# A two-layer gated block, float32, on one core: the residual of the local stage kept by tokens, shared single PSUM banks, new step orders

## The chip, the cores and the metric

The kernel runs on one core of one Trainium2 chip, in float32. The metric is the time of one launch in microseconds, as the device measures it; lower is better. The profile is of one execution, with its instructions on TensorE (PE; its weight loads are PEld), VectorE (DVE), ScalarE (ACT), GpSimd (POOL) and SyncE (SP, which here only issues DMAs), and its DMA packets.

## The reference

Sixteen batches of 256 tokens by 128 features go through two layers, each a gated cross-attention and a gated feed-forward part:

```python
x = x + tanh(g_xattn[0]) * cross_attention_0(layernorm(x), ctx)        # 16 heads of 8, causal, 64 keys
x = x + tanh(g_ffn[0])   * local_net(layernorm(x))
x = x + tanh(g_xattn[1]) * cross_attention_1(layernorm(x), ctx)        # 16 heads of 8, with biases
x = x + tanh(g_ffn[1])   * experts(layernorm(x))

def local_net(y):                                   # two of these one after the other
    h = shift_token(y)      # features 64..127 of token n come from token n - 1 (zero for n = 0)
    q, k, v = split(h @ wqkv, 3)                    # 8 heads of 64
    q, k = rotary(l2norm(q) * qs, l2norm(k) * ks)
    y = y + local_attention(q, k, v) @ wo           # windows of 64 that look one window back
    h = layer_norm(shift_token(y)) * lg + lb
    a, g = split(h @ w1 + b1, 2)                    # 341 wide each
    return y + (a * gelu(g)) @ w2 + b2
```

The experts: sigmoid of `x @ router_w.T` for 8 experts, the best two, their weights made to sum to one; each expert is `relu(x @ w1)**2 @ w2`, four of width 128 and four of width 256. All eight are computed for all tokens, and weighed by a table that is zero for those not chosen.

## The kernel before

One step works on one batch b: 256 tokens, held as two tiles of 128 tokens by 128 features. `x_sb` holds the residual of the whole kernel by tokens (a token on each partition). Three stages follow one another, each a set of streams of small steps:

- **Cross stage 0** (0 to 142 us): startup loads and tables (FIRST, REST and TABLE steps), cross-attention of all batches (CROSS_STEPS), and the first layer norms of the local stage (NORM_STEPS, the first EARLY batches).
- **Local stage** (142 to 856 us): attention of layer 0 (LOCAL_STEPS), its GLU (GLU_STEPS), attention of layer 1, its GLU (LAST_GLU_STEPS).
- **Cross stage 1** with the experts (856 to 1163 us): SECOND_STEPS and EXPERT_STEPS. The experts start while the cross-attention still runs.

The order of the work is not written out by hand. A table line such as `project 4 PE 0.5 share M:add` says: step `project`, lag 4, on PE, planned cost 0.5 us, needs `share`, takes a buffer of class M until `add` has run. For each engine the steps are put in the order of (batch + lag), and, among equals, of the table. `timetable()` then plays this once in Python: an engine's next step is placed when its needs have ended and the buffers it takes are free by the planned costs. `play()` issues all instructions in that order. On the chip each engine runs its own instructions strictly in order and waits at each for its data and buffers; so what a table fixes is each engine's order, and which bank a step gets, not when a step runs.

PSUM in the cross stages has three double banks BIG0 to BIG2 (any user takes a free one) and two single banks: M, for `turn`, `query`, `mturn` and `project`, and O, for `mix` and `router`. In the local stage there are QK, SC and TR (double), VB and OB (single), each with fixed users; the GLU maps its own names onto them by GLU_HOMES.

The steps that the change touches (lines of the kernel before):

- Layer norm, `normed` (L915): `stat` (DVE, L922/923: mean and variance), `rstd` (POOL, L927/928), `offset` (DVE, L931: minus mean times rstd), `apply` (POOL, L940: x times rstd plus offset), `turn` (PE, L902: two 128x128 transposes into PSUM), `turn_out` (ACT, L951).
- `first` (L1165): the layer norm in front of the local stage; its `out` (ACT) copies the transposed result into **yT**, the residual of the local stage, held transposed: features on partitions, tokens along the row.
- Local attention: `shift` (SP, L1261/1262) copies yT by two DMAs into one of three `hbuf`, the upper 64 features one token later; `qk` (PE, L1267) and `value` (L1297) read hbuf as stationary operand; `sin`, `cos` (DVE, L1278), `sums` (L1292), `top` (DVE, L1383/1388), `total` (L1404); `rotate`, `clip`, `norm`, `scale`, `share` on POOL (L1312, L1317, L1329-1334, L1340, L1410); `value_out` (DVE, L1304) and `dma` (SP, L1305/1307) build `vbuf`; `project` (PE, L1445: 4 matmuls of 256 columns); `add` (DVE, L1451) adds to yT.
- GLU: `shift` (POOL, L1245/1246) copies yT into one of two `gbuf`, one token later for the upper features; `hturn` (PE, L902) turns that back to tokens; `stat`, `apply` (DVE, L1484/1485, L1495) read it in PSUM; `rstd` (POOL, L1489/1490); `nturn` (PE), `affine` (ACT, L1505), `up0` to `up2` (PE, L1521), `gelu` (ACT, L1531), `gate` (DVE, L1539), `down` (PE, L1545: 3 matmuls of 256 columns), `out` (DVE, L1551: PSUM plus bias plus yT). In the last GLU `yturn` (PE) turns the sum to tokens and `back` (DVE, L1561) adds it, gated, to x_sb.
- Cross-attention: `score` (PE, L1015-1031), `top` (DVE, L1040), `parts` (DVE), `mturn` (PE, L1062), `score_t` (PE, L1078-1092), `exp` (ACT, L1102), `mix` (PE, L1115), `log` and `inverse` (ACT), `refine` and `share` (DVE), `project` (PE, L1145), `add` (DVE, L1152).
- Experts: `hid0` to `hid2` (PE, L1632, a BIG bank each), `relu`, `square` (ACT), `out0`, `out1` (PE, L1654: 12 matmuls each, for one tile of tokens and all experts, into one BIG bank), `sum0`, `sum1` (DVE, L1662: eight 128x128 multiply-adds onto x_sb each, then the store, L1666).

Of the kernel before, what the change touches and what calls it, by code (L numbers as in the profile page):

```python
# [40 lines left out]
exp0 7 ACT 1.08 score_t pT:mix  # L41
mturn 2 PE 0.25 parts M:mturn_out
mturn_out 6 ACT 0.38 mturn mT:score_t
exp1 7 ACT 1.08 score_t,exp0
turn_out 4 ACT 0.38 turn xnT:query
rstd 2 POOL 1.03 stat
vals 5 POOL 0.32 - V:mix
refine 8 DVE 0.84 inverse
share 8 DVE 0.43 refine oT:project
log 7 ACT 0.38 mix  # L50
stat 2 DVE 0.92 - sm:apply
offset 3 DVE 0.16 rstd
top0 5 DVE 1.2 score
apply 2 POOL 1.02 offset xn:turn
score 1 PE 1.25 query_out,keys BIG:top0 BIG:top1
turn 0 PE 0.4 apply M:turn_out
keys 3 POOL 0.6 - Kd:score+score_t
mix 3 PE 1.8 exp0,exp1,vals O:share
inverse 7 ACT 0.38 log
top1 5 DVE 1.2 score,top0  # L60
parts 5 DVE 0.9 top0,top1 mp:mturn
add 8 DVE 0.48 project
query 0 PE 0.6 turn_out M:query_out
query_out 4 ACT 0.39 query QT:score+score_t
score_t 2 PE 1.2 mturn_out,query_out,keys BIG:exp0 BIG:exp1
project 4 PE 0.5 share M:add
# [3 lines left out]
inverse 6 ACT 0.38 log  # L70
score 6 PE 1.25 query_out,keys BIG:top0 BIG:top1
apply 1 POOL 1.02 offset xn:turn
stat 3 DVE 0.92 - sm:apply
turn 5 PE 0.4 apply M:turn_out
top0 6 DVE 1.2 score
exp0 5 ACT 1.08 score_t pT:mix
mturn_out 4 ACT 0.38 mturn mT:score_t
exp1 5 ACT 1.08 score_t,exp0
mix 8 PE 1.8 exp0,exp1,vals O:share
rstd 0 POOL 1.03 stat  # L80
top1 6 DVE 1.2 score,top0
parts 6 DVE 0.9 top0,top1 mp:mturn
keys 0 POOL 0.6 - Kd:score+score_t
query 5 PE 0.6 turn_out M:query_out
offset 4 DVE 0.16 rstd
add 9 DVE 0.48 project
turn_out 2 ACT 0.38 turn xnT:query
score_t 7 PE 1.2 mturn_out,query_out,keys BIG:exp0 BIG:exp1
refine 8 DVE 0.84 inverse
share 8 DVE 0.43 refine oT:project  # L90
log 5 ACT 0.38 mix
vals 2 POOL 0.32 - V:mix
project 9 PE 0.5 share M:add
query_out 2 ACT 0.39 query QT:score+score_t
mturn 6 PE 0.25 parts M:mturn_out
# [3 lines left out]
hid2 4 PE 1.88 turn_out,hid1 BIG:relu2  # L99
stat 4 DVE 0.92 -  # L100
hid0 3 PE 1.88 turn_out BIG:relu0
prob 8 ACT 0.22 router
rstd 0 POOL 0.95 stat
apply 0 POOL 0.9 offset exn:turn
relu1 7 ACT 1.06 hid1,relu0
# [333 lines left out]
def flamingo_kernel(ctx: ExitStack, tc: tile.TileContext, a: dict, out: bass.AP):  # L439
# [518 lines left out]
    def cross(layer, small, wp, pp):  # L958
# [203 lines left out]
        )  # L1162


    def first(small, wp, pp, xn_tag, acc):  # L1165

        live = {}

# [610 lines left out]
```

## Time and profile before

| | |
|---|---|
| median of 3 runs | 1164.57 us (1163.31 to 1165.63) |
| the profiled execution | 1164.6 us, its span 1162.8 us |
| granted PE clock, mean | 0.989 |

| stage | from | to | us per batch in the steady part |
|---|---|---|---|
| cross stage 0 | 0 | 142 | 7.23 |
| attention, layer 0 | 142 | 427 | 16.18 |
| GLU 0 | 427 | 491 | 5.05 |
| attention, layer 1 | 491 | 775 | 15.72 |
| GLU 1 | 775 | 857 | 5.28 |
| cross-attention 1 | 857 | 950 | 6.74 |
| experts | 950 | 1163 | 11.49 |

The span runs from the first instruction to the last; around it lie the 1.8 us by which the execution's own time is longer. The time per batch is taken between equal steps of neighbouring batches in the trace. A row of a timeline gives the start, the busy time, the engine, the line, the operation with its tiles and shapes, and in square brackets how long the engine stood idle before and whose work ended that. A busy PE is not a PE at its peak, since the ends of pipelined matmuls are modelled.

### The profile page before, as it was taken

The page shows a single profiled execution, that of the slowest core. Times are in us where ns is not written, and L with a number is a line of the kernel's source. Part 1 is how long each engine was busy: PE and PEld are TensorE (multiplying, and loading weights), DVE is VectorE, ACT ScalarE, POOL GpSimd, SP SyncE. Part 2 cuts the span into 40 slices and gives each one's busy share as a digit, 9 for nine tenths or more (in the row PEclk, how much of TensorE's full clock was granted, in tenths as well). Part 3 has the DMA queues.
Part 4 walks back from the last instruction along what each step waited for, and adds up shares of the span by engine and source line. Part 5 has one row for each costly group of instructions (what it writes and reads, how often), then busy time and mean ns, then how long its engine had stood idle before and what let it go on. Part 6 is the DMA issues. An engine that isn't in the chain of part 4 may idle for free.

```text
span 1162.8 us, 28289 instructions
## 1 busy us (share of the span) xinstructions
PE 1080.4 (93%) x11264; PEld 786.3 (68%) x11264; DVE 940.2 (81%) x2088; ACT 734.9 (63%) x1418; POOL 630.9 (54%) x1079
## 2 busy tenths in 40 slices
PE   7999878999999999888999999999979999999997
PEld 5555535766767777655667767677645557999996
DVE  7887679999999856679999999856757884777777
ACT  4555447888888863357888888853335557555462
POOL 5443179999988833258888888733345460111110
PEclk9999989999999999999999999999989999999999
DMA  6400011111111100001111111100000000000000
GB/s 182 143 2 2 10 24 33 33 29 38 37 31 36 29 10 10 1 14 33 37 30 37 38 34 33 29 7 1 1 1 2 2 1 2 12 13 12 13 12 17
DMA packets 29828, 30.02 MB, mean 26 GB/s; under 512 B 4668, under 2 KB 22656, under 8 KB 29696
## 3 DMA queue, kind: packets, MB, share of 16 engines
q1 hardware_dynamic: 28352, 27.56, 9.4%
q8 instruction: 89, 1.46, 0.5%
q10 hardware_dynamic: 1344, 0.66, 0.2%
q14 instruction: 43, 0.35, 0.1%
HBM read 9.33 MB, written 2.10 MB: 10 GB/s over the span
## 4 chain that ended last, share of the span: by engine, by line
PE 70%; DVE 18%; ACT 6%; issue 4%; POOL 1%; DMA 1%; SPq 0%; DVEq 0%; ACTq 0%; POOLq 0%
PE QK L1267 8%; PE e_y L1654 8%; PE e_h_ps L1632 7%; PE po L1115 5%; PE Ag L1521 4%; PE OB L1427 4%; PE TR L1415 3%; PE SC L1374 3%; ACT pr L1397 3%; DVE mx L1383 3%; PE VB L1297 3%; PE OB L1445 3%; PE TR L1346 3%; DVE qn L1278 3%; PE sT L1092 2%
## 5 line engine op out<-in xcount | busy, mean ns | idle before, releaser
L1397 ACT ACTIVATE pr<-SC,mx,rn 128x128 f32<-128x128 f32 x512 | 185.6, 468 | 36.1 <-DVE mx L1388 36.0
L1267 PE MATMUL QK<-wqkv,hbuf 128*128 128x512 f32 x256 | 129.5, 629 | 19.3 <-DVE qn L1278 14.2
L1410 POOL TENSOR_TENSOR pr<-pr,rs 128x1024 f32<-128x1024 f32 x64 | 121.4, 1896 | 14.7 <-DVE rs L1405 11.4
L1662 DVE SCALAR_TENSOR_TENSOR x_sb<-e_y,e_comb,x_sb 128x128 f32<-128x128 f32 x256 | 89.1, 349 | 21.6 <-PE e_y L1654 13.7
L1644 ACT ACTIVATE e_h<-e_h_ps 128x1024 f32<-128x1024 f32 x48 | 49.2, 1025 | 77.2 <-PE e_y L1654 61.8
L1267 PEld LDWEIGHTS QK<-wqkv,hbuf 128*128 128x128 f32 x256 | 44.6, 193 | 77.8 <-issue 40.2
L1654 PE MATMUL e_y<-mw,e_h 128*128 128x128 f32 x768 | 91.8, 277 | 0.0
L1632 PE MATMUL e_h_ps<-e_xnT,mw 128*128 128x256 f32 x384 | 89.8, 383 | 0.2
L1654 PEld LDWEIGHTS e_y<-mw,e_h 128*128 128x128 f32 x768 | 89.2, 192 | 0.7
L1040 DVE TENSOR_REDUCE nm<-sc 128x16 f32<-128x1024 f32 x64 | 75.0, 1214 | 14.2 <-PE sc L1031 14.0
L1275 ACT ACTIVATE sq<-QK 128x1024 f32<-128x1024 f32 x64 | 65.9, 1030 | 31.8 <-ACT pr L1397 9.0
L1312 POOL TENSOR_TENSOR qn<-qn,u 128x512 f32<-128x512 f32 x64 | 81.3, 1271 | 8.6 <-DVE qn L1278 6.0
L1278 DVE TENSOR_TENSOR u<-QK,tab 128x1024 f32<-128x1024 f32 x64 | 76.9, 1201 | 9.3 <-ACT sq L1275 5.4
L1102 ACT ACTIVATE xpT<-sT,penT 128x1024 f32<-128x1024 f32 x64 | 71.3, 1117 | 20.3 <-PE sT L1092 20.3
L1404 DVE TENSOR_REDUCE rs<-pr 128x8 f32<-128x1024 f32 x64 | 77.6, 1212 | 7.9 <-ACT pr L1397 5.3
L1383 DVE TENSOR_REDUCE mx<-SC 128x8 f32<-128x1024 f32 x64 | 77.5, 1212 | 6.3 <-PE SC L1374 6.3
L1313 POOL TENSOR_TENSOR qn<-qn,u 128x512 f32<-128x512 f32 x64 | 81.6, 1275 | 0.0
L1418 ACT COPY pT<-TR 128x1024 f32<-128x1024 f32 x64 | 64.4, 1007 | 24.0 <-PE TR L1415 24.0
L1278 DVE TENSOR_TENSOR qn<-QK,tab 128x1024 f32<-128x1024 f32 x64 | 77.6, 1213 | 1.1 <-ACT sq L1275 1.1
L1292 DVE TENSOR_REDUCE ss<-sq 128x16 f32<-128x1024 f32 x64 | 77.1, 1205 | 1.1 <-ACT sq L1275 1.1
L1632 PEld LDWEIGHTS e_h_ps<-e_xnT,mw 128*128 128x128 f32 x384 | 70.4, 190 | 10.9 <-DVE x_sb L1662 2.7
L1531 ACT ACTIVATE hhg<-Ag,cols 128x256 f32<-128x256 f32 x64 | 28.7, 472 | 72.7 <-PE Ag L1521 36.4
(217 smaller groups left out, 2644.8 us busy)
## 6 DMA issues: line engine op xcount, KB each, us to landing
vbuf<-vbuf SPq DMA_DIRECT2D x96, 128.0 KB
hbuf<-yT SPq DMA_DIRECT2D x32, 64.0 KB
out_dram<-x_sb SPq DMA_DIRECT2D x32, 64.0 KB
hbuf<-yT SPq DMA_DIRECT2D x32, 63.8 KB
wqkv<-in_L_ffn_wqkv_dram SPq DMA_DIRECT2D x2, 768.0 KB
mw<-in_L_ffn_w_dram SPq DMA_DIRECT2D x2, 768.0 KB
w<-in_L_ffn_w_dram SPq DMA_DIRECT2D x2, 341.0 KB
x_sb<-in_x_dram SPq DMA_DIRECT2D x1, 640.0 KB
```

The costliest lines, as they stand in the source:

```text
L1267: nc.tensor.matmul(ps[:, 512 * j : 512 * j + 512], lhsT=hbuf[b % 3][:, W + t * P : W + (t + 1) * P], rhs=wqkv[:, l, 512 * j : 512 * j + 51 ...
L1278: nc.vector.tensor_tensor(work(tag, b, t, [P, 2, LH, LD], 2, wp), live["QK", b, t].rearrange("p (q h d) -> p q h d", q=2, h=LH), tab[:, l, ...
L1292: nc.vector.tensor_reduce(ss, live["sq", b, t].rearrange("p (g d) -> p g d", d=LD), AX.X, ALU.add)
L1312: nc.gpsimd.tensor_add(qg[:, :, 0:32], qg[:, :, 0:32], ug[:, :, 32:64])
L1313: nc.gpsimd.tensor_add(qg[:, :, 32:64], qg[:, :, 32:64], ug[:, :, 0:32])
L1383: nc.vector.tensor_reduce(mx, live["SC", b, t].rearrange("p (g c) -> p g c", c=P), AX.X, ALU.max, negate=True,)
L1397: nc.scalar.activation(pr[:, g, :], live["SC", b, t][:, g * P : (g + 1) * P], AF.Exp, bias=live["mx", b, t][:, g : g + 1], scale=live["rn" ...
L1404: nc.vector.tensor_reduce(rs, live["pr", b, t], AX.X, ALU.add)
L1410: nc.gpsimd.tensor_tensor(pr, pr, rs, ALU.mult)
L1632: nc.tensor.matmul(ps[:, c * S : (c + 1) * S], lhsT=mw1[:, (4 * j + c) * P : (4 * j + c + 1) * P], rhs=live["xnT", b], start=True, stop=True,)
L1654: nc.tensor.matmul(y[:, e * D : (e + 1) * D], lhsT=live["h", b][:, c, t * P : (t + 1) * P], rhs=mw2[:, c, :], start=(c == cs[0]), stop=(c ...
L1662: nc.vector.scalar_tensor_tensor(xt, live[f"y{t}", b][:, e * D : (e + 1) * D], live["comb", b][:, t, e : e + 1], xt, ALU.mult, ALU.add,)
```

## The change

- **The residual of the local stage is kept by tokens**, as `y_sb`. `apply` of the first layer norm writes it directly, so `turn` and `out` of that norm go. Attention gets its transposed, shifted input by `hturn` (two transposes on PE into bank VB) and `hout` (two ACT copies of 64 partitions into hbuf) in place of two DMAs. The GLU gets its shifted input by three SP DMAs from y_sb to gbuf in place of two POOL copies; its `hturn` goes, `stat` and `apply` read gbuf, `yturn` goes.
- `project` and `down` swap their operands, so that results come by tokens: 16 instructions of 128 columns for 8 of 256, and 12 for 6 (a float32 matmul is two instructions of the trace). The bias b2 is loaded as a row on all partitions and added by a new POOL step `bias`; `out` is a plain add.
- **Layer norm without `offset`**: POOL's `apply` subtracts the mean and multiplies by rstd.
- **Single banks**: `turn`, `query`, `mturn`, `mix`, `project` and `router` take M or O, whichever is free.
- **Experts' halves**: `out0` to `out3` compute four experts each, in the order out2, out3, out0, out1; `weigh` (DVE, four a batch) multiplies a half with the weights of its experts in one 128x512 instruction, `gather` (POOL) adds the four products (256, then 128 wide) and then x_sb, with the store after every second. They take the place of 16 multiply-adds.
- **All step tables are new** in order, lags and planned costs.

```diff
 CROSS_STEPS = """
...
-mturn 2 PE 0.25 parts M:mturn_out
...
-offset 3 DVE 0.16 rstd
...
-turn 0 PE 0.4 apply M:turn_out
...
-project 4 PE 0.5 share M:add
+project 5 PE 0.57 share M:add
...
+turn 0 PE 0.4 apply M:turn_out
...
 GLU_STEPS = """
...
-shift 6 POOL 1.25 - hg:hturn
-stat 2 DVE 0.92 hturn
-hturn 0 PE 0.44 shift T:apply
...
+bias 6 POOL 0.5 shift
+shift 5 DMA2 2.8 - hg:apply
+stat 0 DVE 0.92 shift
+out 4 DVE 0.48 down,bias
...
-    yT = resid.tile([P, B, S], F32, tag="yT", name="yT")
-    hbuf = [resid.tile([P, W + S], F32, tag=f"hbuf{i}", name=f"hbuf{i}") for i in range(3)]
+    y_sb = resid.tile([P, B, 2, D], F32, tag="y", name="y_sb")
+    hbuf = [resid.tile([P, S], F32, tag=f"hbuf{i}", name=f"hbuf{i}") for i in range(3)]
...
-                    xn[:, t, :], x[:, t, :], live["rstd", b][:, t : t + 1],
-                    live["off", b][:, t : t + 1], ALU.mult, ALU.add,
+                    xn[:, t, :], x[:, t, :], live["mv", b][:, t, 0:1],
+                    live["rstd", b][:, t : t + 1], ALU.subtract, ALU.mult,
...
-        def shift(b, t):
-            h = hbuf[b % 3]
-            nc.sync.dma_start(h[0:64, W : W + S], yT[0:64, b, :])
-            nc.sync.dma_start(h[64:128, W + 1 : W + S], yT[64:128, b, 0 : S - 1])
+        def hturn(b, t):
+            turn(acc("VB", b, t, 512), y_sb[:, b])
+
+        def hout(b, t):
+
+            h, ps = hbuf[b % 3], live["VB", b, t]
+            nc.scalar.copy(h[0:64, :], ps[0:64, 0:S])
+            nc.scalar.copy(h[64:128, 1:S], ps[64:128, 0 : S - 1])
...
         def project(b, t):
             ps = acc("OB", b, t, 512)
-            for r in range(4):
-                nc.tensor.matmul(
-                    ps[:, 0:S], lhsT=wo[:, l, r, :], rhs=live["oT", b, 0][:, r, :],
-                    start=(r == 0), stop=(r == 3),
-                )
+            for t in range(2):
+                for r in range(4):
+                    nc.tensor.matmul(
+                        ps[:, t * P : (t + 1) * P],
+                        lhsT=live["oT", b, 0][:, r, t * P : (t + 1) * P], rhs=wo[:, l, r, :],
+                        start=(r == 0), stop=(r == 3),
+                    )
...
         def shift(b, _):
-            shifted(yT, b, gbuf[b % 2])
...
+            g, y = gbuf[b % 2], y_sb[:, b]
+            nc.sync.dma_start(g[:, :, 0:64], y[:, :, 0:64])
+            nc.sync.dma_start(g[1:P, :, 64:D], y[0 : P - 1, :, 64:D])
+            nc.sync.dma_start(g[0:1, 1, 64:D], y[P - 1 : P, 0, 64:D])
...
+        def bias(b, _):
+            y = y_sb[:, b]
+            nc.gpsimd.tensor_tensor(y, y, b2[:, l].unsqueeze(1).to_broadcast([P, 2, D]), ALU.add)
...
         def out_(b, _):
-            nc.vector.scalar_tensor_tensor(
-                yT[:, b, :], live["B", b][:, 512 : 512 + S], cols[:, 16 + l : 17 + l],
-                yT[:, b, :], ALU.add, ALU.add,
-            )
...
+            y = y_sb[:, b].rearrange("p t d -> p (t d)")
+            nc.vector.tensor_add(y, live["B", b][:, 512 : 512 + S], y)
...
-        def sum_(b, t):
...
+        def weigh(b, j):
+            t, half = j // 2, j % 2
+            nc.vector.tensor_tensor(
+                work(f"w{j}", b, [P, 4, D], 4, wp, tag="e_w"),
+                live[f"y{t}", b][:, 512 * half : 512 * half + 512]
+                .rearrange("p (e d) -> p e d", e=4),
+                live["comb", b][:, t, 4 * half : 4 * half + 4].unsqueeze(2)
+                .to_broadcast([P, 4, D]), ALU.mult,
+            )
+
+        def gather(b, j):
+            w, xt = live[f"w{j}", b], x_sb[:, 2 * b + j // 2, :]
+            nc.gpsimd.tensor_add(w[:, 0:2, :], w[:, 0:2, :], w[:, 2:4, :])
+            nc.gpsimd.tensor_add(w[:, 0, :], w[:, 0, :], w[:, 1, :])
+            nc.gpsimd.tensor_add(xt, xt, w[:, 0, :])
+            if j % 2:
+                nc.sync.dma_start(out_v[:, 2 * b + j // 2, :], xt)
...
-    anywhere = lambda r, b: accs if r == "BIG" else (r,)
+    anywhere = lambda r, b: accs if r == "BIG" else ("M", "O") if r in ("M", "O") else (r,)
```

The orders that come of the new tables, as far as the prediction speaks of them (k is the batch of the round). Cross stage 0, PE: mix k, query k+3, score_t k+1, project k-1, turn k+4, score k+3, mturn k+2. Local attention: `hturn` stands behind `turn0` on PE, `hout` behind `root1` on ACT; POOL runs clip, rotate, share, norm, scale. GLU 0: DVE runs gate0 k, out k-1, gate1 k, apply k+3, gate2 k, stat k+4; PE runs nturn k+1, up2 k-1 ahead of up0 k, up1 k, down k-1. GLU 1: DVE runs gate0 k, back k-2, out k-1, stat k+3, gate1 k, gate2 k, apply k+3; PE runs nturn k+2, up0 k+1, down k, up1 k+1, up2 k+1. At the end of each attention layer DVE runs top0 of batch 15, stat 0, value_out1, add 13, apply 0, stat 1, total0 of batch 15, top1, apply 1, stat 2, apply 2, total1; SP issues shift 0 and shift 1 between the last batch's first and second `vbuf` copies.

## The prediction

> **What bounds the kernel now.** I read five views in this order. First the page's busy line and the shares of the chain that ended last:
>
> ```profile
> PE 1080.4 (93%) x11264; PEld 786.3 (68%) x11264; DVE 940.2 (81%) x2088; ACT 734.9 (63%) x1418; POOL 630.9 (54%) x1079
> ...
> PE 70%; DVE 18%; ACT 6%; issue 4%; POOL 1%; DMA 1%; SPq 0%; DVEq 0%; ACTq 0%; POOLq 0%
> ```
>
> PE carries the end, but not alone. So, second, the table of stretches, one of steady batches per stage (columns: length, then busy PE, PEld, DVE, ACT, POOL, clock, DMA):
>
> ```profile
> 28.26:122.19 93.93, 86.35 (x1431) 51.64 (x1434) 76.31 (x222) 51.16 (x91) 37.16 (x88) 1.00 0.14 48
> ...
> 442.00:482.00 40.00, 36.03 (x176) 29.21 (x175) 25.10 (x80) 14.65 (x32) 13.00 (x32) 1.00 0.01 3
> 790.00:840.00 50.00, 47.22 (x228) 35.22 (x227) 33.94 (x104) 16.27 (x37) 16.69 (x40) 1.00 0.00 1
> 553.15:616.06 62.91, 62.91 (x754) 44.34 (x753) 60.75 (x69) 53.20 (x114) 51.84 (x72) 1.00 0.16 35
> ...
> 1000.00:1140.00 140.00, 139.75 (x952) 129.22 (x951) 103.00 (x432) 75.76 (x97) 20.80 (x46) 1.00 0.04 13
> ```
>
> The first cross stage (first line) leaves PE idle 7.6 of 94 us, GLU 0 (second) 10%, GLU 1 (third) 6%; local attention (fourth) has PE and DVE full together; the experts (last) are PE alone. Third, timelines of one batch show who makes PE wait. In the first cross stage:
>
> ```profile
> 89.90 0.71 PE L1145 MATMUL pw<-wT,oT 128*128 128x128 f32 x4
> 91.19 0.27 PE L1062 MATMUL mT_ps<-ident_bf,mparts 128*128 128x128 bf16 x2 [0.57 <-DVE x_sb L1152]
> ```
>
> `mturn` has all its data, but its bank M is held by `project` until DVE's `add` has read it. GLU 0 has the same picture with bank B and `out`:
>
> ```profile
> 460.23 0.48 DVE L1551 SCALAR_TENSOR_TENSOR yT<-Bg,cols,yT 128x256 f32<-128x256 f32 x1
> ...
> 460.76 1.09 PE L1521 MATMUL Bg<-hnTg,w 128*85 128x256 f32 x4 [0.50 <-DVE yT L1551]
> ```
>
> Among the experts the bank of the first `out` goes to `hid1` only after eight DVE sums, so the second `out` (same 24 instructions) is stretched from 2.68 to 2.94 us until its successor may start; and at the end 24 sums stand behind PE's last matmul, which ends at 1154.2:
>
> ```profile
> 1067.43 2.92 PE L1654 MATMUL e_y<-mw,e_h 128*128 128x128 f32 x24
> 1070.37 1.99 PE L1632 MATMUL e_h_ps<-e_xnT,mw 128*128 128x256 f32 x8
> ```
> ```profile
> 1151.29 8.97 DVE L1662 SCALAR_TENSOR_TENSOR x_sb<-e_y,e_comb,x_sb 128x128 f32<-128x128 f32 x24
> ```
>
> Fourth and fifth, the waits and the DMA records, used below.
>
> **The change, part by part.** Base: the profiled execution, 1164.6 us (span 1162.8 and 1.8 around it); the median, 1164.57, is the same.
>
> *Cross stage 0.* 13 batches take 93.93 us: 7.23 each. With M and O open to any user, `mturn` waits for no `add`. Late next: `turn` takes the bank that `share` frees, so a loop score to tops 2.39, `parts` 1.07, `refine` .91, `share` .40, `turn` .36, `score` 1.42: 6.55, and six handovers of about .03 make 6.75. PE's own work is 6.5, ACT's loop 6.55. Gain .48 x 13 = 6. Bounds: 0 (`share` to `turn` costs what `add` to `mturn` did, the nearest row) to .7 x 13 = 9 (PE dense).
>
> *Start of the local stage.* After the first `qk` at 142.2 PE waits until 148.1 for `n.turn[2]`, behind POOL's `apply`s, each waiting for DVE's `offset`. `apply` now writes y_sb and needs no PE; `hturn` of the first batches has its data from the previous stage. The second `sin` goes from 152.6 to about 149.8 and the third from 160.0 to 155: gain 4 (bounds 0 and 6).
>
> *Local attention.* PE gets `hturn` (two transposes, .25 us by the L902 rows) and `project` 16 x .112 = 1.79 in place of 1.72; ACT gets `hout`, two 64-partition copies, .7 by its 128x256 copies of .38, on 13.3 of 15.7 us, where it idled .8 and .5. The two SP copies to hbuf go. Layer 1 has no spare PE time (62.91 of 62.91) but its 15.72 us contain waits on DVE: I take +.2 x 16 = +3 (bounds 0, +.35). Layer 0 now pays 16.18 a batch (201.81 to 331.29, 8 batches), since `n.turn` and `n.out` run beside it; they go, so does `offset`: -.2 x 8 = -1.5. Sum +1.5, bounds -5 and +8. DVE's L1388 takes .17 us alone and .74 to 1.06 when it ends with POOL's share L1410: the new POOL order (clip, rotate, share, norm, scale) could move that either way by .4 a batch, which is inside the bounds.
>
> *GLU 0.* Bank B is freed by `out`, which no longer stands behind two gates: chain up2, up0, up1 (.87 each), down 1.34, `out` .79 (.2 to its start, .47, .12 back to PE) = 4.74 against 5.05. `down` keeps its time (12 half-width instructions for 6). Gain .31 x 13 = 4.
>
> *GLU 1.* Before, 5.28: `hturn`, `nturn` and `yturn` are three pairs of transposes, and gates queue. After, PE holds nturn .22, three ups 2.61, down 1.34 = 4.17; the loop up1, gelu1, gate1, down, with bank A for up0, about 4.4. Gain .85 x 13 = 11 (bounds 4, 14). POOL's `bias` (128x256, broadcast) .76 by L983 and `rstd` .95 fit in 4.4.
>
> *The GLU's shift.* It was two POOL copies (.39 + .40); now three SP copies with rows of 256 bytes, two buffers. The nearest row is hbuf's second copy, L1262: issue at 201.85, first packet at 203.06, landed at 203.84, 2.0 us. Three issues .5 apart give 1.0 + 1.7 = 2.8 us, and all is hidden. But the second copy has 127 rows. SP's queue shows 3672 packets of 4 bytes, the completion marks. 227 copies with 16 engines each make 3632; the other 40 come out exactly if a copy uses the largest divisor of its row count up to 16: 8 for the router's 8 rows, 7 x 2 and 8 x 1 for the small rows, and 5 (not 16) for each of the two loads of 85 rows. 127 is prime: one engine gets all 254 packets. Packets of 256 bytes follow each other on one engine at 14.3 ns (qk_scale loads); for SBUF to SBUF the 1024-byte packets take 44 ns at first and 70 when all engines run, 1.6 times as long, so 14.3 to 22.7. Landing: .51 + 1.21 + 254 x 14.3 ns + .35 = 5.7 us, or 7.8. I take 5.7, since one engine alone is like the first packets.
>
> Does that hide? On DVE in GLU 0 two periods hold `stat` to the next `apply` but one (3.2 by its rows) and the copy with its two handovers: (3.2 + 5.7 + .25) / 2 = 4.6, under 4.74; in GLU 1 (2.75 + 5.95) / 2 = 4.35, under 4.4. So it is just covered, with no slack. The bound of the engine itself is 254 packets and some .35 for the other two copies: 4.0 at 14.3 ns, 6.1 at 22.7. At the two transitions it is not covered: `stat[0]` and `stat[1]` stand on DVE between the last batch's `top0`, `total0` and `top1`; shift[0] is issued after the last `value_out0` (401.4 + 1.1) and lands at 408.4, shift[1] behind it on the same engine at 412.3, while `total0[15]` started at 410.74: 413.3 now. I take +2.5 each, +5 (bounds 0, +10).
>
> [...] By the nearest row alone (16 engines) the sum below would be 5 lower. [...]
>
> *Transitions otherwise.* GLU 0 to layer 1: a DMA round of 2 us becomes transpose and copy, 1 us: -1. GLU 1 to the second cross stage: `yturn` goes: -1.
>
> *Cross stage 1.* Period 6.74, the same gap at `mturn`; the loop mix, query, score_t, exp0, turn_out, exp1 is 6.45: -.3 x 10, and expert work that starts earlier fills gaps: -4 together (bounds 0, -8).
>
> *Experts.* 11.49 a batch. PE content: 3 `hid` x 1.73, turn .22, router .37, 2 x 2.68 = 11.14. `weigh` (128x512, .69 by L1304 .67) frees a half at once; 4 gathers x 1.3 us (POOL: 256 wide .62, 128 wide .35 twice) = 5.2 fit in 11.1. -.3 x 13 = -4 (bounds 0, -6).
>
> *Tail.* 8.6 us after PE's end become .15 + .69 + 1.3 + up to 1 in a queue + 2.4 for the store (1160.3 to 1162.8) = 5: -3.5.
>
> Sum: -6 - 4 + 1.5 - 4 - 11 + 5 - 2 - 4 - 4 - 3.5 = -32, so 1164.6 - 32 = **1132.6 us**.
>
> **Rivals.**
> 1. *Only the banks fail*: in both cross stages `share` to `turn` takes the place of the wait removed, and the change doesn't do there what it says. The gap of .57 at `mturn` speaks for it, the new order (turn behind project) against. -6 and -3 gone: 1141.6.
> 2. *Local attention pays*: `hturn` takes bank VB between the values, `hout` sits in ACT's row of exps, and the loop DVE to PE lengthens by .6 x 32 = 19, at most what `n.turn` cost layer 0 in its worst cycle, 1.6 us (17.33 against 15.72): 1151.6.
> 3. *The shift binds both GLUs (slower)*: if packets take 22.7 ns, one engine needs 6.1 us a batch: the 15 saved there are lost, (6.1 - 5.05) x 16 + (6.1 - 5.28) x 16 = 30 come on top, and 4 at the transitions: 1132.6 + 15 + 30 + 4 = 1181.6. Break-even: the sum can bear 32 us, 15 by lost gains and 17 by .53 a batch, 5.7 us, from 21 ns on.
> 4. *More comes*: the upper bounds of both cross stages (-3, -4), of the start (-2), of GLU 1 (-3) and the experts (-2), and GLU 0 at PE's own 4.2 (-7): 1111.6.
>
> **Numbers.** Forecast 1132.6 (1123 to 1141 as its own range) .48; rival 1 .12; rival 2 .13; rival 3 .12; rival 4 .15. Range: 1108 (rival 4 and a little) to 1158 (rival 2 with bounds of the local part); outside are rival 3 and a tenth of the rest. .2% (2.3 us) is about what a measurement of this kernel can tell from no change. Faster .86, within .02 (between rivals 2 and 3), slower .12.
>
> **What would show it.** In the new profile: no PE gap at `mturn`, cross period 6.75; GLU periods 4.7 and 4.4, with DVE's `stat` not waiting for a DMA; if it does, rival 3, and the period is the packet count times the packet time. Local cycles within 15.7 to 16.0. DVE's last `weigh` under 1 us after PE's last matmul. I am wrong if the local cycles exceed 16.4, if the copy lands in 3 us, or in more than 7.

## The result and the profile after

The changed kernel takes **1172.49 us** (median of 4 runs, 1170.80 to 1173.91) against 1164.08 us of the kernel before beside it (4 runs): a ratio of 1.006, 95% interval 1.0036 to 1.0084. It is slower, by a little over half a per cent, where 1132.6 was forecast; the time lies above the range. Run once more later (label s9_same, 12 runs), it took 1169.67 us, ratio 1.0032 (1.0019 to 1.0046): slower again.

The page of the changed kernel's profiled execution (span 1170.3 us, before 1162.8) has these lines where the prediction showed those of before; first busy time, then the shares of the chain that ended last:

```profile
PE 1080.1 (92%) x11648; PEld 809.9 (69%) x11648; DVE 897.7 (77%) x1832; ACT 747.3 (64%) x1466; POOL 777.7 (66%) x1239
...
PE 57%; DVE 11%; POOL 7%; DMA 4%; ACT 4%; issue 4%; SPq 2%; POOLq 0%; DVEq 0%; ACTq 0%
```

DVE got 42 us of work less, as meant. But POOL got 147 us more (630.9 to 777.7). The chain after can be followed back no further than 139.65 us, so its shares add up to 89%, and the two lines can't be compared as they stand. Summed from 140 us on in both traces, PE holds 669 us of the chain (696 before) and DVE 124 (199), while POOL, DMA and SP's queue (SPq) hold 148 together, where they held 14. The work was taken from an engine and a wait that were near the bound, and what came in its place got onto the path.

Where the 7.5 us of span went is read between the same steps of both traces (the `add` of a cross stage, the `add` of attention, the GLU's `out`), which leaves nothing over:

| stretch | before, us | after, us | difference | forecast |
|---|---|---|---|---|
| start to the last add of cross stage 0 | 140.7 | 135.2 | -5.5 | -6 |
| to the last add of layer 0 (local start, attention, transition) | 287.9 | 307.1 | **+19.2** | -3 |
| to the last out of GLU 0 | 88.3 | 80.3 | -7.9 | -4 |
| to the last add of layer 1 | 259.7 | 264.7 | +5.0 | +4.5 |
| to the last out of GLU 1 | 78.9 | 72.6 | -6.3 | -11 |
| to the first add of cross stage 1 | 28.8 | 29.7 | +0.9 | -1 |
| to the end (cross stage 1, experts, tail) | 278.6 | 280.7 | **+2.1** | -11.5 |
| sum | 1162.8 | 1170.3 | +7.5 | -32 |

Five groups of lines show why. **One: the clock at the local start.** The stretches 140 to 198 us before and after (columns: length, busy PE, PEld, DVE, ACT, POOL, granted clock, DMA share, GB/s). Before:

```profile
140.00:198.00 58.00, 43.86 (x369) 25.15 (x368) 49.49 (x77) 32.88 (x69) 46.82 (x80) 0.91 0.11 26
```

After:

```profile
140.00:198.00 58.00, 42.02 (x270) 22.11 (x270) 42.14 (x63) 28.24 (x59) 47.05 (x74) 0.74 0.07 14
```

PE is as long busy with a quarter fewer matmuls: 0.74 of the clock instead of 0.91. In the clock's own records, PE ran at half speed for 30.7 us there, in pieces of 3.4 us and multiples of it; before, for 10.2 us. The pieces differ from run to run: in s9_same, the same kernel, 17 us and a clock of 0.85, and the first add of layer 0 came 67.9 us after the last one of the cross stage, not 74.4 (before: 62.7).

**Two: POOL's `apply`.** Groups of POOL's instructions (columns: busy us, mean ns of one). Before:

```profile
L940 POOL TENSOR_SCALAR n_xn<-x_sb,n_rstd,n_off 128x128 f32<-128x128 f32 x32 | 14.1, 448 | 1.6 <-DVE n_off L931 0.7 <-PE n_xnT_ps L902 0.7
```

After:

```profile
L939 POOL TENSOR_SCALAR y_sb<-x_sb,n_mv,n_rstd 128x128 f32<-128x128 f32 x32 | 25.5, 803 | 0.0
```

The same shape, the same engine, two operations in both; but subtract-and-multiply takes 803 ns where multiply-and-add took 448: 0.70 us more a batch, in each of four norms (cross stage 0, local, cross stage 1, experts).

**Three: PE waits inside the experts.** A timeline of one batch after (start, busy, engine, line, and in brackets the idle time before and who ended it):

```profile
1105.55 0.69 DVE L1659 TENSOR_TENSOR e_w<-e_y,e_comb 128x512 f32<-128x512 f32 x1 [1.72 <-PE e_y L1651]
...
1106.29 4.73 PE L1651 MATMUL e_y<-mw,e_h 128*128 128x128 f32 x40 [0.51 <-DVE e_w L1659]
```

Before `out3` PE stands 0.51 us, until `weigh2` has read `out2`. The experts' period rose from 11.49 to 11.88 us.

**Four: the GLU's shift binds GLU 1.** The chain of waits there (start, length, what):

```profile
803.22 0.03 issue
803.25 0.65 SPq L1473
...
803.94 5.56 DMA gbuf<-y_sb
...
809.60 0.30 DVE stg L1481
...
811.63 1.01 DVE hng L1492 x2
...
814.13 2.76 SPq L1475
...
818.45 5.39 DMA gbuf<-y_sb
```

SP issues, the copy lands, `stat`, `rstd` and `apply` follow, and only then has the buffer room for the next but one copy. PE is not on this chain at all. From 803.22 to the next copy's start at 812.66 are 9.44 us for two batches (two buffers): 4.72, and the period is 4.71 (a mean: single cycles take 4.43 to 5.4).

**Five: the tail.** PE's last matmuls and POOL's last `gather`, after:

```profile
1150.01 10.88 PE L1651 MATMUL e_y<-mw,e_h 128*128 128x128 f32 x96
...
1165.94 0.72 POOL L1669 TENSOR_TENSOR e_w<-e_w 128x256 f32<-128x256 f32 x1
1166.74 0.45 POOL L1670 TENSOR_TENSOR e_w<-e_w 128x128 f32<-128x128 f32 x1
1167.27 0.45 POOL L1671 TENSOR_TENSOR x_sb<-x_sb,e_w 128x128 f32<-128x128 f32 x1
```

PE runs the `out`s of the last two batches in one go, eight in 10.88 us, 1.36 each; POOL takes 1.74 for each `gather`. From PE's end at 1160.9 to the end of the span are 9.4 us (before 8.6).

### The profile page after: what moved, and what is told of

Read it like the earlier page. It is cut to its first block, busy times and chain, and to the rows that moved or that the text cites. A ratio compares the mean times of both kernels' runs of the same rounds, so it can differ in the third digit from the quotient of the medians.

```text
span 1170.3 us, 29244 instructions
## 1 busy us (share of the span) xinstructions
PE 1080.1 (92%) x11648; PEld 809.9 (69%) x11648; DVE 897.7 (77%) x1832; ACT 747.3 (64%) x1466; POOL 777.7 (66%) x1239
## 4 chain that ended last, share of the span: by engine, by line
PE 57%; DVE 11%; POOL 7%; DMA 4%; ACT 4%; issue 4%; SPq 2%; POOLq 0%; DVEq 0%; ACTq 0%
PE QK L1260 9%; PE e_y L1651 7%; PE e_h_ps L1626 7%; DMA gbuf<-y_sb 4%; PE OB L1420 4%; PE TR L1408 4%; PE TR L1339 4%; PE SC L1367 4%; PE OB L1439 4%; PE VB L1290 3%; PE Ag L1518 2%; PE po L1114 2%; PE Bg L1518 1%; PE SC L1354 1%; DVE qn L1271 1%
## 5 line engine op out<-in xcount | busy, mean ns | idle before, releaser
L1390 ACT ACTIVATE pr<-SC,mx,rn 128x128 f32<-128x128 f32 x512 | 185.8, 473 | 20.6 <-DVE mx L1381 20.5
L1260 PE MATMUL QK<-wqkv,hbuf 128*128 128x512 f32 x256 | 133.8, 648 | 22.5 <-DVE qn L1271 21.6
L1659 DVE TENSOR_TENSOR e_w<-e_y,e_comb 128x512 f32<-128x512 f32 x64 | 42.6, 688 | 84.4 <-PE e_y L1651 79.9
L1268 ACT ACTIVATE sq<-QK 128x1024 f32<-128x1024 f32 x64 | 65.7, 1026 | 30.9 <-ACT pr L1390 11.8
L1669 POOL TENSOR_TENSOR e_w<-e_w 128x256 f32<-128x256 f32 x64 | 46.4, 725 | 57.3 <-DVE e_w L1659 57.3
L1339 PEld LDWEIGHTS TR<-ident,qn 128*128 128x128 f32 x512 | 58.6, 143 | 28.0 <-issue 17.9
```

Source lines behind the costliest of these rows:

```text
L1260: nc.tensor.matmul(ps[:, 512 * j : 512 * j + 512], lhsT=hbuf[b % 3][:, t * P : (t + 1) * P], rhs=wqkv[:, l, 512 * j : 512 * j + 512], star ...
L1339: nc.tensor.transpose(ps[:, i * P : (i + 1) * P], qf[:, i * P : (i + 1) * P], ident)
L1390: nc.scalar.activation(pr[:, g, :], live["SC", b, t][:, g * P : (g + 1) * P], AF.Exp, bias=live["mx", b, t][:, g : g + 1], scale=live["rn" ...
```

## The experiments

Each kernel is the changed one with one edit, unless said otherwise. The kernel before took 1166.04 us beside s1 to s4, 1166.12 beside s5 to s8 and 1166.09 beside s9 to s12, so the medians stand against one another, and against 1169.67 of the changed kernel in s9_same. Ratios are to the kernel before, with 95% intervals. "Start" is the time from the last add of cross stage 0 to the first add of layer 0.

### s1_rows: the shift's copy on more engines

```diff
-            nc.sync.dma_start(g[1:P, :, 64:D], y[0 : P - 1, :, 64:D])
+            nc.sync.dma_start(g[1:113, :, 64:D], y[0:112, :, 64:D])
+            nc.sync.dma_start(g[113:P, :, 64:D], y[112 : P - 1, :, 64:D])
```

> The changed kernel with the GLU shift's second copy cut into 112 rows and 15 rows; all else as it is. Theory: 127 rows run on one DMA engine, 254 packets at 14 ns, 5.4 us from issue to landing, and this lengthens the two transitions from attention to GLU (add of batch 14 to add of batch 15 and the one before: 15.68 and 14.70 us where the kernel before has 10.84) and GLU 1 (4.68 us a batch). With 16 and 15 engines the copies land in about 3.5 us, GLU 1 falls to 4.4 to 4.45 a batch (-3.5), the transitions lose 6 to 8 us together, the half-clock stretches near 420 and 765 us go: 1160 to 1164 us in all. GLU 0 stays at 4.68, since there the copy is covered. Rival: the GLU and the transitions are bound by the new orders (stat ahead of top and total on DVE), not by the landing: then the landing falls and the time stays within 3 us of 1172. Second rival: the number of rows does not set the engines; then the landing stays over 5 us.

Measured: 1160.35 us, 0.9954 (0.9938 to 0.9971). The period of GLU 1 falls from 4.71 to 4.43, the two long cycles of each transition from 14.36 and 15.68 to 12.87 and 13.11 us (layer 1: from 15.06 and 14.70 to 12.99 and 13.26); GLU 0 stays (4.67). The chain of waits in GLU 1 is now PE's alone:

```profile
784.98 0.22 PE Ng L907 x2
785.20 1.13 PE Ag L1519 x4
786.33 1.34 PE Bg L1548 x12
787.66 0.88 PE Ag L1519 x4
788.54 0.86 PE Bg L1519 x4
```

These five make 4.43, the period. So the copy of 127 rows did sit on one engine, and that, not the bytes, was what GLU 1 and the transitions waited for. In the changed kernel's DMA records its 254 packets of 256 bytes stand one behind the other, from 456.47 to 460.17 us: 3.70 us, 14.6 ns each; one packet of 4 bytes stands behind them, where the copy of 128 rows just before has 16 (455.92 to 456.07 us). SP's issues change too: the third, which took 2.5 to 2.8 us behind the copy of 127 rows in GLU 1, takes 0.91 in this run, and the fourth 0.60.

### s2_forms: four ways to write the apply

Every norm gets another form: cross stage 0 subtract and multiply, but with the mean copied to a compact tile first; the local norm multiply and subtract; cross stage 1 add and multiply; the experts multiply and add.

```diff
+            if label == 0:
+                nc.gpsimd.tensor_copy(off, m)
+                s, ops = (off, r), (ALU.subtract, ALU.mult)
+            elif label == "n":
+                nc.gpsimd.tensor_tensor(off, m, r, ALU.mult)
+                s, ops = (r, off), (ALU.mult, ALU.subtract)
+            elif label == 1:
+                nc.gpsimd.tensor_scalar_mul(off, m, -1.0)
+                s, ops = (off, r), (ALU.add, ALU.mult)
+            else:
+                nc.vector.scalar_tensor_tensor(off, m, -1.0, r, ALU.mult, ALU.mult)
+                s, ops = (r, off), (ALU.mult, ALU.add)
```

> The changed kernel with four forms of the layer norm's apply on POOL, one for each of its four uses, to find why one 128x128 apply takes 0.79 us where it took 0.44. Cross stage 0: (x - mean) * rstd with the mean copied into a tile of its own; start of the local stage: x * rstd - mean * rstd; cross stage 1: (x + (-mean)) * rstd; experts: x * rstd + offset, as before the change. If the strided mean is the cause, all four take 0.44. If any subtract is, the first two take 0.79 and the last two 0.44. If only subtract as the first operation is, the first alone takes 0.79. If the order (add or subtract ahead of the multiply) is, the first and third do. In time: two or three small POOL instructions of 0.2 more a batch, a long apply less; if apply's 0.7 us a batch is what layer 0 pays (16.3 us a batch against 16.06), layer 0 falls by 3 us in all and the start of the local stage by 1 to 2: 1167 to 1170. If POOL's time has cover there, no change beyond 2 us.

Measured: 1171.11 us, 1.0041 (1.0022 to 1.006). The groups of POOL over the whole span:

```profile
L953 POOL TENSOR_SCALAR y_sb<-x_sb,n_rstd,n_off 128x128 f32<-128x128 f32 x32 | 25.3, 797 | 1.7
...
L953 POOL TENSOR_SCALAR e_xn<-x_sb,e_rstd,e_off 128x128 f32<-128x128 f32 x32 | 14.2, 453 | 12.3 <-DVE e_off L950 9.0 <-PE e_h_ps L1639 3.2
```

Both cross stages share one group, so they are read from windows of their own: 801 ns with subtract in cross stage 0, 456 ns with add in cross stage 1. The compact mean changes nothing (801), nor does the place of the subtraction. It is the subtract itself that costs POOL 0.35 us a tile. DVE shows no such price: its apply in the GLU, subtract and multiply of the same shape, has a median of 340 ns (with add and multiply, in s12, 346).

### s3_weigh: `weigh2` only after `out3`

```diff
-weigh2 7 DVE 0.69 out2,route w:gather2
+weigh2 7 DVE 0.69 out3,route w:gather2
```

> The changed kernel with the first weigh of each tile placed after both halves of out instead of between them. Theory: the two halves are one tile to the program's dependences, so the second half (out3) waits for the weigh that reads the first (0.51 us idle on PE in every batch, period 11.88 us). Placed after it, PE has no gap there, the period is 11.37, and some 13 batches give -6.5 us: 1166. Rival: the wait is for the bank or for DVE's route, and comes back at the next matmul: period 11.8 or more, less than 1.5 us gained. A loss is possible at the end, where gathers are POOL's queue: +0.5 at most.

Measured: 1163.30 us, 0.998 (0.9964 to 0.9997). The gap is gone, both weighings now come together:

```profile
1097.91 4.71 PE L1651 MATMUL e_y<-mw,e_h 128*128 128x128 f32 x40
1100.05 1.29 DVE L1659 TENSOR_TENSOR e_w<-e_y,e_comb 128x512 f32<-128x512 f32 x2 [3.65 <-PE e_y L1651]
```

The period falls from 11.88 to 11.20 (11.49 before the change: the forecast 0.3 less), and the stretch from the first add of cross stage 1 to the end from 280.7 to 273.2 us. `out2` and `out3` write the two halves of one double bank, which is one tile of the program. The trace before the edit shows `out3` waiting for `weigh2`, so the tile has one set of waits: in the order out2, weigh2, out3 the second half waits for the reader of the first, which it does not touch. The edit lets one step start later and gains 7.5 us in that stretch.

### s4_warm: twelve matmuls more, to hold the clock

Before some of the first `qk` steps of layer 0, 12 matmuls of 512 columns are added whose result nothing uses.

```diff
+            fill = {(0, 0): 1, (0, 1): 3, (1, 0): 3, (1, 1): 2, (2, 1): 1, (3, 0): 2}
+            for i in range(fill.get((b, t), 0) if l == 0 else 0):
+                nc.tensor.matmul(
+                    acc("OB", b, t, 512), lhsT=ident, rhs=wqkv[:, 0, 0:512],
+                    start=True, stop=True,
+                )
```

> The changed kernel with twelve matmuls of 128x512 more, whose results nobody reads, put in front of the first qk steps of layer 0 where PE idles. Theory: the local stage starts 11.6 us slower than before (last add of cross stage 0 to first add of layer 0: 74.3 us against 62.7) because PE is idle enough there that it runs at half clock for 31 us from 140 to 195 us, against 10 us before, and qk (3.1 to 3.8 us at half clock, 1.95 at full) stands on the chain qk, sin, cos, next qk. With the fill the clock stays full for all but one or two of the 3.4 us stretches, the first add comes 6 to 10 us earlier, 1163 to 1167 in all. Rival: POOL's longer apply and the new orders set the start, the low clock only follows: the clock rises, the first add moves by less than 2 us, and the matmuls added cost up to 3.

Measured: 1165.91 us, 1.0 (0.9984 to 1.0015). The start becomes 63.3 us, and the stretch 140 to 198 us has a full clock and 407 matmuls instead of 270:

```profile
140.00:198.00 58.00, 50.96 (x407) 28.53 (x406) 49.30 (x77) 36.83 (x79) 52.65 (x84) 1.00 0.09 20
```

In the changed kernel PE stands idle there four times for 3.1 to 3.6 us between matmuls; with the added ones no gap is over 1.5 us. So with PE busy for 50.96 of the 58 us, where it was 42.02, the granted clock is 1.00 and not 0.74, and 4 us of the kernel come back. But 63.3 is not below the 62.7 of before: of the gain of 4 that was forecast for the start nothing is seen, even at full clock. The chain of waits of this kernel there runs through POOL (`clip`, `rotate`, `scale`, the norm's `rstd` and `apply`, `share`, one behind the other), where that of before ran mostly through DVE and PE (from 140 to 200 us, POOL holds 23.8 us of this chain and 4.4 of that before).

### s5_add: the apply as addition and multiplication

```diff
+            less = work("less", b, [P, 2])
+            nc.gpsimd.tensor_scalar_mul(less, live["mv", b][:, :, 0], -1.0)
             for t in range(2):
                 nc.gpsimd.tensor_scalar(
-                    xn[:, t, :], x[:, t, :], live["mv", b][:, t, 0:1],
-                    live["rstd", b][:, t : t + 1], ALU.subtract, ALU.mult,
+                    xn[:, t, :], x[:, t, :], less[:, t : t + 1],
+                    live["rstd", b][:, t : t + 1], ALU.add, ALU.mult,
```

> The changed kernel with apply on POOL as (x + (-mean)) * rstd, with one POOL instruction more a batch for -mean (0.25 us); all else as it is. Apply falls from 1.58 to 0.90 us a batch, so POOL has 0.45 less net in each. Theory: POOL is nearly full in layer 0 (it was busy 118.9 of 129.5 us before the change), and the longer apply is what takes layer 0 from 16.06 to 16.3 to 16.7 us a batch, with PE gaps that bring the clock down near 235 us; with the short form layer 0 is at 16.1 or less, no half clock inside it, and the start is 1 to 2 us shorter: 1172 falls to 1165 to 1169. Rival: hturn and hout set layer 0's cycle (layer 1, which has no apply, is at 15.8 against 15.74 before, so they cost only 0.07): layer 0 stays above 16.3 and the total within 2 us.

Measured: 1164.29 us, 0.9986 (0.9973 to 1.0). Each apply now costs 0.89 us for its two tiles and 0.24 for the negation, 0.45 less a batch. The period of cross stage 1 falls from 6.57 to 6.37. The first eleven cycles of layer 0 average 16.51 us (16.71 in s9_same, 16.31 in the changed kernel's first profile, 16.06 before): the apply takes at most 0.2 of the 0.65 by which they are longer than before, so that part of the expectation failed.

### s6_tail: the last batch's gathers on DVE

```diff
-            nc.gpsimd.tensor_add(w[:, 0:2, :], w[:, 0:2, :], w[:, 2:4, :])
-            nc.gpsimd.tensor_add(w[:, 0, :], w[:, 0, :], w[:, 1, :])
-            nc.gpsimd.tensor_add(xt, xt, w[:, 0, :])
+            on = nc.vector if b == B - 1 else nc.gpsimd
+            on.tensor_add(w[:, 0:2, :], w[:, 0:2, :], w[:, 2:4, :])
+            on.tensor_add(w[:, 0, :], w[:, 0, :], w[:, 1, :])
+            on.tensor_add(xt, xt, w[:, 0, :])
```

> The changed kernel with the last batch's gathers on DVE instead of POOL; all else as it is. Theory: at the end PE runs the out steps of batches 14 and 15 one after the other (10.9 us), and POOL, with 1.74 us a gather, is 6.8 us behind PE's end (9.4 us from PE's last matmul to the end of the span; I had 1.3 us a gather and 5 us). With batch 15 on DVE the two engines share them, PE's end to the end is 4.5 to 5.5 us: -4 to -5. Rival: DVE's adds on SBUF wait for POOL's running adds (as its L1388 row did, 0.17 alone and up to 1.06 beside POOL's work), so that the gain is 2 or less.

Measured: 1168.36 us, 1.0023 (1.0011 to 1.0035); the end comes 7.8 us after PE's last matmul instead of 9.4. Now DVE is the queue: 0.68 for `weigh` and 0.43, 0.29 and 0.29 for the sums are 1.7 us for each `out` of 1.36. POOL's queue was the tail, but moving the last batch's four gathers whole to one other engine gains only 1.6. The rival's number came, though mostly not for its reason: only the first of these gathers on DVE is slower (0.97, 0.43 and 0.50 us), the others wait for one another.

### s7_all: the five edits together

s1, s3, s4, s5 and s6 in one kernel.

> The changed kernel with all the single edits together: the copy cut into 112 and 15 rows, weigh behind both halves, the fill of the clock at the start, apply with add, the last batch's gathers on DVE. If the causes are separate, their gains add up: copy -7 (transitions 4, GLU 1 -4.5, of 12 measured some 4 is where the clock's stretches fell), weigh -7.5, clock -6.5, apply -4, tail -4: 1172.5 - 29 = 1143 (1139 to 1149), 2% under the kernel before. If the clock is the common cause behind several (fewer half-clock stretches counted twice), the sum is only partly there: 1149 to 1156.

Measured: **1138.82 us** (1137.26 to 1140.22), 0.9776 (0.976 to 0.9792): 2.2% faster than the kernel before, and 30.9 us faster than the changed kernel in s9_same. The five gains measured alone add up to 26.2 us (9.3, 6.4, 3.8, 5.4 and 1.3), so together they are worth at least as much as one by one; the difference is not clear of the noise, as the same 1169.67 enters all five gains. Start 63.6 us, GLU 1 4.43, cross stage 1 6.37, first add of cross stage 1 to the end 269.2. Against the kernel before that is -27 us, where -32 was forecast, and the time lies within 1123 to 1141, the forecast's own range: costs of this kind had taken the place of the gain.

### s8_fixed: the banks M and O fixed again

The changed kernel with `mturn`, `turn`, `query`, `project` on M alone, and `mix`, `router` on O alone; orders as in the change.

```diff
-    anywhere = lambda r, b: accs if r == "BIG" else ("M", "O") if r in ("M", "O") else (r,)
+    anywhere = lambda r, b: accs if r == "BIG" else (r, r) if r in ("M", "O") else (r,)
```

> The changed kernel with the single banks fixed again: turn, query, mturn and project in M, mix and router in O; new orders as they are. It prices the sharing alone. Theory (as in the prediction): sharing removes the wait of a step on PE for the add that frees project's bank; without it a cross batch has that gap again, 6.87 becomes 7.2 to 7.5 in stage 0 and 6.57 becomes 6.8 to 7.1 in stage 1: +5 to +12 in all. Rival: the gain of the cross stages came from the new orders alone (turn behind project, add a round later): then the periods stay within 0.1 us and the total within 2.

Measured: 1195.93 us, 1.0268 (1.0248 to 1.0287). The period of cross stage 0 is 7.35 instead of 6.87, that of cross stage 1 7.72 instead of 6.57, and from its first add to the end 299.9 us pass instead of 280.7. PE's timeline here in cross stage 0:

```profile
84.83 0.71 PE L1144 MATMUL pw<-wT,oT 128*128 128x128 f32 x4
86.21 0.41 PE L907 MATMUL xnT_ps<-ident,xn 128*128 128x128 f32 x2 [0.67 <-DVE x_sb L1151]
```

And in the changed kernel:

```profile
81.20 0.71 PE L1144 MATMUL pw<-wT,oT 128*128 128x128 f32 x4
82.12 0.41 PE L907 MATMUL xnT_ps<-ident,xn 128*128 128x128 f32 x2 [0.20 <-DVE oT L1137]
```

With M fixed, `turn` behind `project` waits 0.67 us for `add` to read M; with a free choice it waits 0.20 for `share` to free the other bank, the wait that the prediction had named as next. With these orders the sharing is worth 26 us; the mechanism was right, the size is far above what was expected (+5 to +12). 7 us of it lie in cross stage 0, whose period is longer here than before the change (7.24), and 19 behind the first add of cross stage 1. That the new order, with `turn` right behind `project`, makes the fixed banks so dear is likely, but not shown: no run has the old orders with shared banks.

### s9_same: the changed kernel once more

> The changed kernel as it is, once more, so that the runs of this call have it beside them. The start of the local stage (last add of the cross stage to the first add of layer 0) is what I look at: 74.4 us in its first profile, with 30.6 us of half clock between 140 and 195, but 66 to 68 in three other kernels that do the same work there. Theory (the long start is the clock's doing and varies): near 67 here, with less half clock, and a median of 1166 to 1173. Rival (it belongs to this kernel): 74 again, and 1172.

Measured: 1169.67 us, 1.0032 (1.0019 to 1.0046), start 67.9 us. The long start of 74.4 belonged to that execution's clock, as the theory said; the other runs bear it out (s10 and s12, which have another order, left aside): with no half clock in the start it takes 63 us (s4, s7), with 7 to 21 us of it 66 to 69, with 30.7 us 74.4. But start and layer 0 together hardly moved: 304.0 us from the last add of cross stage 0 to the last of layer 0 (307.1 before that, 287.9 in the kernel before), because the first two cycles became longer (17.71 and 19.47 us) as the first add came earlier. They are to be judged together.

### s10_dve and s12_all2: the first norm's apply on DVE

s10 is the changed kernel with the edit, s12 is s7 with it (there as addition and multiplication).

```diff
-apply 1 POOL 0.9 rstd
+apply 1 DVE 0.6 rstd
...
+            on = nc.vector if dest is not None else nc.gpsimd
             for t in range(2):
-                nc.gpsimd.tensor_scalar(
+                on.tensor_scalar(
```

> The first layer norm of the local stage (batches 0 and 1 ahead of it, 14 in it) is applied by DVE (same two operations, one table line: apply on DVE, planned 0.6 us) instead of POOL. Theory: what took the place of DVE's offset at the start is POOL's queue: its chain there is clip, rotate, norm, rstd, apply, share one behind the other (rows 0.27, 1.27, 1.27, 1.04, 1.0, 1.58, 1.9), and apply holds 1.58 of each batch. Without it the first add of layer 0 comes 4 to 6 us earlier than about 67 (so 61 to 63), the cycles of the first seven batches of layer 0 shrink from 16.0 to 18.1 to below 16.5, and the median falls by 8 to 12 against the unchanged kernel of this call. Rival: DVE, which gets 0.9 us a batch more (0.45 twice by the row of the GLU's apply on DVE), is as full there; then the start stays near 66 and layer 0 stays above 16.3, and the median moves by less than 4.

> All five edits, and in addition the first layer norm applied by DVE (as addition and multiplication, the small negation on DVE too). If POOL's queue is what the start and the first cycles of layer 0 wait for: start 60 to 62 (from 63.6), first seven cycles of layer 0 below 16.5 (from 16.0 to 19.0), 1128 to 1134. Rival (DVE as full): 1136 to 1142.

Measured: s10 1177.22 us, 1.0088 (1.0061 to 1.0115); s12 1152.65 us, 0.9884 (0.9861 to 0.9908), 14 us slower than s7. My theory, that POOL's queue alone makes the start and the first cycles long, falls; worse than the rival. In s12 the start is 68.4 us (63.6 in s7) though the clock is nearly full (0.989 over the whole run). Nine of its first eleven cycles of layer 0 take 15.2 to 16.9 us, evener than before the edit (15.2 to 19.0); but two, 22.03 and 21.18 us, are far longer, and so are two in s10 (20.70 and 20.05), where PE's `hturn` waits 6.3 us in two pieces for the apply on DVE. DVE's timeline in s10 at the first of them:

```profile
276.03 0.70 DVE L940 TENSOR_SCALAR y_sb<-x_sb,n_mv,n_rstd 128x128 f32<-128x128 f32 x2
...
277.46 1.30 DVE L940 TENSOR_SCALAR y_sb<-x_sb,n_mv,n_rstd 128x128 f32<-128x128 f32 x2
...
282.09 0.59 DVE L940 TENSOR_SCALAR y_sb<-x_sb,n_mv,n_rstd 128x128 f32<-128x128 f32 x2
```

Three applies, with two batches' `stat` between them, stand within 7 us in a queue that has no idle time there, in the order that the planner found for the new engine. A step moved to DVE changes the order of all of DVE; so these two runs show that the move costs, and not whether POOL's queue would be worth relieving in another way.

### s11_nofill: s7 without the twelve matmuls

> The kernel with all five edits but without the 12 filler matmuls. If they hold the clock of the start also there, where apply is short: 4 to 7 us slower than the one with all five, 1143 to 1146, with half clock between 140 and 195. Rival: with the short apply PE is dense enough by itself: under 2 us slower, 1139 to 1141.

Measured: 1143.24 us, 0.9816 (0.9791 to 0.984): 4.4 us slower than s7. PE is at half clock for 20.5 us from 140 us on, and the start is 67.5 us instead of 63.6. The fillers are worth 4 us in the best kernel too; the shorter apply alone does not hold the clock there.

## Why the prediction was wrong, step by step

**Right.** *Cross stage 0*: -6 forecast, -5.5 measured, period 6.87 for 6.75, and the next wait is the one named (`turn` on `share`); s8 shows it by undoing it. (The bound "PE's own work is 6.5" is 6.64 by the row shown, 86.35 us for 13 batches.) *GLU 0*: 4.68 for 4.74, the shift hidden there; that the stretch gained 7.9 and not 4 is luck, since 3.4 of it lie in the last three cycles, for which no term stood. *The 127 rows on one engine*: as worked out, with 14.6 ns a packet for 14.3.

**Right by luck.** *Layer 1*: the stretch measured +5.0 for +4.5, but from other terms. The steady cycles alternate between 15.2 and 16.3 and average 15.76 for 15.74, so the +3 for `hturn` and `hout` did not come (+0.2 over twelve cycles); the last three cycles cost 3.8 where 2.5 was taken, and the way from GLU 0 to the first add 1.0 where -1 was taken.

**Wrong, by weight:**

1. *"Start of the local stage ... gain 4 (bounds 0 and 6)"* and *"Layer 0 ... -1.5"*. Measured, start and layer 0 with its transition: +19.2, in s9_same +16.1, against -3. The step that failed is the one that let PE's old wait go and took the next `sin` from it, without asking what POOL's queue and the clock do with a thinner start. The transition is 4.5 of it (s1 takes 4.1 off those cycles), the clock 4 (s4, s11), the apply some more (s5: start and layer 0 together 301.0 for 304.0). In s7, with all of these mended, 292.9 us are left against 287.9: 0.9 in the start, the rest in the first five cycles (85.6 for 81.3). That rest of 5 us has no run that takes it away: s10 and s12 were to settle it and did not. The first five cycles in s7, before the change, and in s12 (columns as above):

```profile
198.20:283.78 85.58, 80.42 (x990) 59.10 (x989) 76.40 (x102) 68.69 (x149) 78.71 (x125) 0.98 0.11 25
...
203.40:284.68 81.28, 79.08 (x951) 56.65 (x950) 79.96 (x117) 68.09 (x146) 74.98 (x114) 1.00 0.15 34
...
203.75:291.60 87.85, 82.76 (x992) 60.67 (x991) 84.31 (x122) 69.44 (x151) 70.11 (x103) 0.96 0.11 24
```

Before, DVE was full (80.0 of 81.3 us). In s7 DVE has 9 us to spare, while POOL has 3.7 us of work more and the cycles are 4.3 longer, with POOL busy for 92% as before. That fits POOL's queue as their limit, but doesn't show it, for with `apply` on DVE it is DVE that is full (84.3 of 87.9). My condition "local cycles exceed 16.4" was met in early cycles of layer 0 (up to 18.1, in s9_same 19.5), not in the steady ones, which alternate between 15.2 and 16.3.
2. *Experts: "weigh frees a half at once", -4.* A half counts for nothing by itself: the two halves are one tile for the waits, and PE's second `out` waited for the `weigh` of the first. +0.39 us a batch instead of -0.3; s3 gives 7.5 us of that stretch for one word in the table. I had counted the instructions and not looked at which tile the order makes wait for which.
3. *`apply` was priced at nothing*: I took POOL's row of multiply-and-add as if the pair of operations did not matter. 0.70 us a batch in four norms; s5, which takes back 0.45 of it, is worth 5.4 us.
4. *GLU 1: "4.4", measured 4.71, and the transitions, +5 taken, +8.3 measured.* The mechanism (one engine, just covered) was right, the landing mis-sized: from the first issue to landing 5.7 us were taken, and 6.3 (803.22 to 809.50) and 6.9 (816.95 to 823.84) were measured, once 7.4 (793.14 to 800.52), past the 7 that I had named as proof of error. The packets were right; the two issues take 0.65 and 0.70, not 0.5, and SP's third issue, 2.76 us, stood before the next copy's first one. "No slack" was the word that should have widened this term. Rival 3 had GLU 1 right, GLU 0 and its price, slow packets, wrong.
5. *Tail: "= 5: -3.5"*, measured 9.4. A `gather` is 1.74, not 1.3 us, and it is not one that is left after PE's end but the queue of two batches, since PE runs the last eight `out`s without `hid` between them (1.36 us each). The term "up to 1 in a queue" should have been the sum of eight differences, 8 x (1.74 - 1.36) = 3.0, which with 1.74 for the `gather` gives 8.0; the rest is that the first of the eight gathers starts only at 1153.72, 3.7 us after PE's first matmul of that stretch, behind two `out`s and a `weigh`.

*Cross stage 1* (-0.3 a batch) measured -0.17, and -0.37 once the apply is short (s5); that term was right without the third point. Two errors are the size of an instruction on POOL (`apply`, `gather`); the others lie in a queue, a wait or the clock, which a change of order or form moved.

## What to carry to other kernels

An operation is priced by a row of the same engine, shape and operators; here a row that differed in one operator was wrong by a factor of 1.8 (803 ns for 448). Where a change takes a wait away, walk through the queue of every engine that gets more work, and ask which tile, not which half of it, the next instruction waits for. Before giving up a change that measures as a small loss, take its costs out one by one: here five edits of a few lines turned +0.3% to +0.6% into -2.2%.

## What the runs showed of the hardware

- GpSimd's 128x128 float32 instruction with two per-partition operands took 0.80 us when one of its two operations was a subtract (803 ns in the changed kernel, 797 and 801 in s2), and 0.45 to 0.46 with add and multiply, in either order (448 ns before, 453 and 456 in s2, 0.89 us for two in s5); a compact mean did not help (801 ns, s2). VectorE showed no such difference (medians of 0.34 us with subtract in s10, 0.35 with add in s12).
- With twelve matmuls more, TensorE's granted clock was 1.00 from 140 to 198 us, at the start of the local stage, with PE busy for 50.96 (s4) and 51.52 us (s7) of the 58. In the changed kernel without them it was busy for 42.02, with idle gaps of 3.1 to 3.6 us, at a clock of 0.74. Without them it ran at half speed there for 7 to 31 us (the changed kernel, s3, s9, s11), by the changed kernel's records in pieces of 3.4 us and multiples of it.
- The copy of 127 rows issued by SyncE left 254 packets of 256 bytes one behind the other, 14.6 ns each, and one packet of 4 bytes behind them, where a copy of 128 rows left 16: the work of one DMA engine. The issue that followed it held SP for 2.5 to 2.8 us. With the copy cut into 112 and 15 rows, the two issues behind the 112 rows took 0.91 and 0.60 us (s1): the long issue went with the copy on one engine. What it waited for there is not shown by these runs.
